# Norms moved to ScalarE, stores moved to the Sync queue, and weight fetches given out at each product's head

## The chip, the cores and the metric

The kernel runs on one core of one Trainium2 chip. Its engines are TensorE (PE, with PEld for the loading of weights), VectorE (DVE), ScalarE (ACT), GpSimd (POOL) and SyncE (SP). Each has its own in-order queue. DMAs are given out by SP, ACT or POOL, and an engine that gives one out first waits, in its queue, for what that DMA must wait for. The metric is the device time in microseconds of one launch.

## The reference

One block of a network on 4096 tokens of width 256, in float32: linear attention without a softmax, a residual and a layer norm, then a feed-forward part with a second residual and layer norm.

```
energy  = K^T V                       # 64 x 64, over all tokens
x1      = layernorm(x + (Q energy) * sqrt(3/64) @ wo^T)
h       = silu(x1 @ w1^T * s1) * (x1 @ w2^T * s2)        # 1024 wide
h       = gelu(h @ h1^T * hs1)                           # 1024 x 1024
h       = gelu(h @ h2^T * hs2)                           # 1024 x 1024
out     = layernorm(x1 + h @ w3^T * s3)
```

All the w and h matrices of the feed-forward part hold only -8, 0 and 8, which is what lets the kernel work with sums of their blocks without loss.

## The kernel before, in words

The tokens are eight tiles of 512, worked on in four pairs (p = 0 to 3). Values that need full precision are held as two parts, hi and lo (`convert`: a cast on ACT, L231, and a subtraction on DVE, L232), and every product is done once with each.

Stages. Keys, values and energy of all tiles come first, then queries. `stack` builds for each tile an operand `stk` of queries, hi over lo; for tiles 3 to 5 the lower half is made by `stack_lo` (L550) from a copy `qf`. Then tile 0 and tile 1 get their attention (`attention_out`, L137 and L138), the residual (`add`, L158), statistics, root and norm (`attend_norm`: `stats`, `root` with a power on POOL at L86, `norm` at L167), a turn on PE and the gate products (`gate_products`, L611; `gate`, L620 and L621), 16 gates through a ring of three pairs of banks. Gates 6, 7, 9 and 10 are followed by sums of blocks of h1; gates 11 and 14 by `add` for tiles 2 and 3, whose x comes from `load_x`.

Square layers (`square_layer`). Each of h1 and h2, times the 1024 x 1024 operand of a pair of tiles, is done with seven products of 512 x 512 in place of eight. A `product` is 32 matmuls (L278); it takes two half blocks of weights, `ws`, from a list `held`. The seven weight operands, in the order of use, are A11, A12, S2, S1, S3, A22, S4: three blocks of h and four sums of blocks (`sums`), which the kernel itself forms on DVE from raw blocks (`raw_blocks`) and stores (`store`, L440) to a scratch tensor `sw` in HBM. `fetch` keeps five half blocks in five rotating buffers, so a fetched block waits for the product that last read its buffer. In the first pair A11, A12 and A22 are fetched from h by POOL (L267, with a cast to the type of the products), the sums from `sw` by SP (L269); later pairs take all from `sw`, to which `copy` (L260) brings the A blocks.

Spare work is handed out by `fill`: after the third to sixth product of a layer it takes jobs from the list `background` until a budget in microseconds is used up (FILL; FIRST for the first layer of the first pair). In that first layer the jobs are the sums of h2 (`second_sums(k)`, k0 to k3, each two parts; the second part orders the raw block k+2), and for tiles 2 and 3 statistics, roots and norms on POOL (a0, a1 and b0, b1 of `attend_jobs`), then block transposes on DVE (L815; a2, a3 and b2, b3). A transposed tile is then moved block by block to `xT` by 32 DMAs a tile (`move`, L216), half on SP and half on POOL, 14 behind each product. Order written in the code is the order of each queue, as the schedule is manual.

After the two layers come the products with w3 (`last_products`, L755), the second residual (`take`), and the norm that goes to the output. A dummy activation `once` loads the table of Silu for the next pair's gates.

Of the kernel before, what the change touches and what calls it, by code (L numbers as in the profile page):

```python
# [11 lines left out]
F32 = mybir.dt.float32  # L12
# [9 lines left out]
P = 128  # L22
# [22 lines left out]
def block_kernel(ctx: ExitStack, tc: tile.TileContext, a: dict, out: bass.AP):  # L45
# [103 lines left out]
    def attend_norm(t, x, ps, pool):  # L149

        mv = p2.tile([P, NS, 2], F32, tag="mv1", name=f"mv1_{t}")
        y = pool.tile([P, NS, E], F32, tag=f"x2_{t // 2 % 2}", name=f"x2_{t}", bufs=2)
        r = {}
        x2[t] = y

        def add(g, j=slice(0, 2)):
            u = x[:, 2 * g : 2 * g + 2, :][:, j, :]
            nc.vector.tensor_tensor(u, u, ps[g][:, j, :], ALU.add)  # L158

        def stats(g):  # L160
            norm_stats([x[:, 2 * g + j, :] for j in range(2)], mv, 2 * g)

        def root(g):
            r[g] = rstd_of(p2, mv[:, 2 * g : 2 * g + 2, :], "a", 2)

        def norm(s, engine=nc.vector):
            engine.tensor_scalar(  # L167
                y[:, s, :], x[:, s, :], mv[:, s, 0:1],
                r[s // 2][:, s % 2 : s % 2 + 1], ALU.subtract, ALU.mult,
            )  # L170

        return add, stats, root, norm

    def turn_on_pe(t, slot):
# [61 lines left out]

    MOVES = 14
    FILL = {2: 2.0, 3: 4.0, 4: 1.5, 5: 3.5}
    FIRST = {2: 2.8, 3: 5.4, 4: 2.8, 5: 5.4}

    PLACE = {A11: (0, 0), A12: (HK, 0), A22: (HK, T)}
    ORDER = [A11, A12, S2, S1, S3, A22, S4]
# [27 lines left out]
            held.append(w)  # L270

    def product(ps, part, start):
        for h in range(2):
            w = held.popleft()
            for o in range(2):
                for k in range(HK):
                    for i in range(2):
                        nc.tensor.matmul(  # L278
                            ps[2 * h + o], w[:, k, o * P : (o + 1) * P], part[i][:, k, :],
                            start=start and k == 0 and i == 0, stop=k == HK - 1 and i == 1,  # L280
                            skip_group_check=True,
                        )
        fetch()
        products[0] += 1
        if products[0] in COPY:
            copy()
        move(MOVES)
# [5 lines left out]
    owed = [0.0]  # L293
    checks_due = [0]

    def fill(us):

        if checks_due[0] > 0:
            checks_due[0] -= 1
            check_job()  # L300
            us -= 1.4
        owed[0] = min(owed[0] + us, us)
        while background and owed[0] > 0:
            cost, job = background.popleft()
            owed[0] -= cost
            job()
        if not background:
            owed[0] = 0.0

    def square_layer(xb, first, sc, tail, spare):  # L310
# [58 lines left out]
        fill(spare[4])  # L369
        for o in range(HK):  # L370
            nc.scalar.copy(bb[:, o], al[o])  # L371
        for o in range(HK):
            c22(o)

# [2 lines left out]
        fill(spare[5])  # L377
        for o in range(HK):
            gelu(b5[:, o], al[o], HK + o)

        product(be, x22, False)
        n2 = convert(b5)
# [38 lines left out]
            )  # L421
        return d

    def sums(layer, k, raw):
        a11, a21, a12, a22 = (raw[:, i, :].bitcast(F32) for i in range(4))
        if layer == 0 and k < 2:

            so = [
                p1.tile([P, HK, T // 2], FR, tag="ws", name=f"so{layer}", bufs=HELD)
                .rearrange("p k o -> p (k o)").rearrange("p (m o) -> p m o", m=2)  # L430
                for _ in range(2)
            ]
        else:
            so = [
                p1.tile([P, 2, T], FR, tag="so", name=f"so{layer}", bufs=2) for _ in range(2)
            ]
        v = [s[:, i, :] for s in so for i in range(2)]

        def store(i):
            nc.gpsimd.dma_start(  # L440
                out=sw[layer][2 * i : 2 * i + 2, :, :, k, :].rearrange("m h p o -> p m h o"),
                in_=so[i].bitcast(F32).rearrange("p m (h o) -> p m h o", h=2),
            )

        def first():
            plus(v[0], a21, a22)
            plus(v[1], v[0].bitcast(F32), a11, ALU.subtract)
            store(0)

        def second():  # L450
            plus(v[2], a11, a21, ALU.subtract)
            plus(v[3], a12, v[1].bitcast(F32), ALU.subtract)
            store(1)

        return first, second
# [91 lines left out]
            nc.scalar.copy(qf[t][D:P], pq[t][D:P])  # L547

    def stack_lo(t):
        nc.gpsimd.tensor_tensor(  # L550
            stk[t][D:P], qf[t][D:P], stk[t][D:P].bitcast(F32), ALU.subtract
        )

# [3 lines left out]
    for t in range(NT):  # L557
        keys_values(t)
        if t > 0:
            energy(t - 1)  # L560
        if NT - 1 - EARLY <= t < NT - 1:
            queries(t - NT + 1 + EARLY)
            stack(t - NT + 1 + EARLY)
        if t >= NT - 4:
            if t % 2 == 0:
                early = sums(0, t // 2 - 2, raws[t // 2 - 2])
            early[t % 2]()
    queries(2, (0,))
    energy(NT - 1)
# [29 lines left out]
    split(0, 2)  # L599
    norm(2)  # L600
    norm(3)
    for t in range(3, LATE):
        stack_lo(t)
    for t in range(LATE, NT):
        stack(t)

# [19 lines left out]
    for o in range(3):  # L626
        for ps, w in zip(ring[o], (w1, w2)):
            gate_products(ps, w, o, slot, 0, slice(0, T // 2))
        if o == 1:
            turn(2, 4)  # L630
            split(2, 4)
    for o in range(3):
        for ps, w in zip(ring[o], (w1, w2)):
            gate_products(ps, w, o, slot, 0, slice(T // 2, T))
# [15 lines left out]
    for i in range(3, 2 * KH):  # L650
# [20 lines left out]
                later = sums(0, i // 3, raws[i // 3])  # L671
            later[i % 3]()
        if i == 7:
            raw_blocks(1, 0, xTr, nc.gpsimd)
            xs[2] = load_x(2)
            xs[3] = load_x(3)
        if i in (4, 14):
# [7 lines left out]
    def second_sums(k):  # L685
# [6 lines left out]
        def end():  # L692
            both[1]()
            if k + 2 < HK:
                raw_blocks(1, k + 2, later_raws[k % 2], nc.gpsimd)

        return [(1.4, begin), (1.4, end)]

# [101 lines left out]

        return [(1.3, functools.partial(half, s)) for s in (0, 2)]

    def attend_jobs(t):

        add, stats, root, norm = steps[t]

        def half(g):
            stats(g)
            root(g)
            for s in (2 * g, 2 * g + 1):  # L810
                norm(s, nc.gpsimd)

# [60 lines left out]
    for p in range(NP):  # L873
        ta, tb = 2 * p, 2 * p + 1
        if p > 0:
            first = []
            ask(1)
            for i in range(2 * KH):
# [21 lines left out]
                    fill(1.2)  # L900
                if p == NP - 1 and i in (11, 13, 15):
                    bounds((i - 11) // 2)
        if p + 1 < NP:
            (a0, a1), (a2, a3) = attend_jobs(ta + 2)
            (b0, b1), (b2, b3) = attend_jobs(tb + 2)
            if p == 0:
                k0, k1, k2, k3 = (second_sums(k) for k in range(HK))
                background.extend((*k0, *k1, a0, a1, *k2, *k3, b0, b1, a2, a3, b2, b3))
            else:
                background.extend((a0, a1, b0, b1, a2, a3, b2, b3))  # L910
        tail = lambda: None
        for layer, sc in enumerate((hs1, hs2)):
            if p + layer > 0:
                ask(4 if p else 1)
            if p == NP - 1 and layer == 1:
                background.append((1.4, functools.partial(bounds, 3)))
            xb, first, tail = square_layer(
                xb, first, sc, tail, FILL if p + layer else FIRST
            )
        while background:  # L920
            background.popleft()[1]()
        if p + 1 < NP:
            nc.scalar.activation(once, mhalf[:, :1], AF.Silu)

        made = {}

        for s in range(NS):
            last_products(0, first[0], s)
        move(MOVES)
        tail()  # L930
        made[2] = convert(xb[3])
        for s in range(NS):
            last_products(1, first[1], s)
# [231 lines left out]
```

## Time and profile before

| What | Value |
| --- | --- |
| median of 3 runs | 653.18 us (652.52 to 653.35) |
| the profiled execution, its own time | 653.67 us |
| its span, first to last instruction | 651.9 us |
| PE busy | 631.8 us (97%) |
| DVE busy | 496.1 us (76%) |
| ACT busy | 381.4 us (59%) |
| POOL busy | 233.1 us (36%) |
| PE's share of the chain of work that ended last | 86% |
| granted TensorE clock, mean | 0.987 |

In a row of the group table stand the line, the engine, the operation, what it writes from what, the count, then busy time and mean nanoseconds of one, then the idle time of the engine just before such instructions and what ended it. In the chain and the timelines a row is: start in us, length in us, what ran, and how many of them (a timeline adds the idle time before, in brackets). The chain is followed back from the last instruction, each time to what released it. Matmuls overlap, so their mean of 391 ns is longer than the distance between two of them.

### The profile page before, as it was taken

Reading aid. Unit: us, or ns where it says so; the run is one execution under the profiler, and the core shown is the slowest. Engines: PE = TensorE matmul, PEld = TensorE weight load, DVE = VectorE, ACT = ScalarE, POOL = GpSimd, SP = SyncE. Lnnn points to the kernel's source line nnn. Section 1 sums busy time; section 2 is a strip of 40 time slices with the busy share of each in tenths; the row PEclk is TensorE's granted clock in tenths of the full one; section 3 lists DMA queues with packets and bytes.
Section 4 is the critical chain, followed back from the end, with each engine's and each line's share of the span. In section 5 each row is a group of like instructions: output and inputs, shape, how many; then the busy total and the mean of one; then the engine's idle time right before and its main releaser. Section 6 shows DMA issues by size and latency. Waiting matters only on the chain.

```text
span 651.9 us, 8976 instructions
## 1 busy us (share of the span) xinstructions
PE 631.8 (97%) x3163; PEld 533.6 (82%) x3163; DVE 496.1 (76%) x750; ACT 381.4 (59%) x522; POOL 233.1 (36%) x290
## 2 busy tenths in 40 slices
PE   8999999959999999999999999999999999999994
PEld 7878888848898888888898888888899888888894
DVE  3789986895475888698677988798767987588466
ACT  5546472645664455655684556766684556766564
POOL 1234117722814713632535722631645720000005
PEclk9999999979999999999999999999999999999998
DMA  8988749845853037764762125654860125644201
GB/s 335 330 300 246 244 144 364 268 155 182 250 152 103 33 137 247 268 218 167 225 191 71 60 97 171 216 183 154 248 190 4 65 98 173 215 150 141 98 1 67
DMA packets 58800, 113.44 MB, mean 174 GB/s; under 512 B 19488, under 2 KB 34528, under 8 KB 58368
## 3 DMA queue, kind: packets, MB, share of 16 engines
q1 hardware_dynamic: 40864, 73.56, 34.0%
q0 software_dynamic: 17520, 38.55, 18.6%
q10 hardware_dynamic: 368, 0.72, 0.3%
q8 instruction: 26, 0.43, 0.3%
q14 instruction: 22, 0.18, 0.1%
HBM read 97.08 MB, written 18.87 MB: 178 GB/s over the span
## 4 chain that ended last, share of the span: by engine, by line
PE 86%; DMA 5%; DVE 5%; POOL 1%; issue 1%; ACT 1%; SPq 0%; POOLq 0%; DVEq 0%; ACTq 0%
PE bank L278 53%; PE bank L611 18%; PE bank L755 9%; DMA sw<-so 3%; PE bank L507 2%; DVE f L290 2%; PE bank L528 1%; DMA ws<-in_h 1%; POOL x L167 1%; DVE so L290 1%; DMA f<-in_xt 1%; PE bank L518 1%; PE bank L137 1%; PE bank L138 1%; DVE lo L232 1%
## 5 line engine op out<-in xcount | busy, mean ns | idle before, releaser
L278 PE MATMUL bank<-hi,ws 128*128 128x512 f32 x896 | 350.3, 391 | 7.7 <-DMA ws<-in_h 7.7
L278 PE MATMUL bank<-lo,ws 128*128 128x512 f32 x896 | 349.9, 391 | 0.0
L232 DVE TENSOR_TENSOR lo<-f,hi 128x1024 fp32r<-128x1024 f32 x144 | 170.3, 1221 | 69.6 <-ACT hi L231 69.1
L278 PEld LDWEIGHTS bank<-hi,ws 128*128 128x128 f32 x896 | 169.0, 189 | 43.3 <-DVE f L290 8.1
L278 PEld LDWEIGHTS bank<-lo,ws 128*128 128x128 f32 x896 | 169.1, 189 | 35.2
L231 ACT CAST hi<-f 128x1024 fp32r<-128x1024 f32 x144 | 144.5, 1051 | 52.0 <-PE bank L278 26.9
L318 ACT ACTIVATE f<-f,hs 128x512 f32<-128x512 f32 x96 | 62.8, 715 | 71.7 <-DVE f L290 71.7
L611 PE MATMUL bank<-hi,w 128*128 128x512 f32 (+1 forms) x268 | 101.7, 383 | 1.0 <-DVE d L766 0.6
L611 PE MATMUL bank<-lo,w 128*128 128x512 f32 (+1 forms) x268 | 101.2, 381 | 0.1
L620 ACT ACTIVATE f<-bank,s 128x512 f32<-128x512 f32 x64 | 44.0, 690 | 65.6 <-PE bank L611 62.3
L290 DVE TENSOR_TENSOR f<-f,f 128x1024 f32<-128x1024 f32 x64 | 76.5, 1221 | 4.5 <-ACT f L318 3.8
L290 DVE TENSOR_TENSOR f<-f,bank 128x512 f32<-128x512 f32 x96 | 62.1, 681 | 21.8 <-ACT f L371 16.0
L767 POOL TENSOR_TENSOR x<-x,d 128x256 f32<-128x256 f32 x31 | 27.0, 897 | 114.0 <-DVE d L766 113.9
L621 DVE SCALAR_TENSOR_TENSOR f<-bank,s,f 128x512 f32<-128x512 f32 x64 | 47.7, 748 | 26.2 <-PE bank L611 23.6
L755 PE MATMUL bank<-w,lo 128*128 128x256 f32 x256 | 61.6, 283 | 0.0
L755 PE MATMUL bank<-w,hi 128*128 128x256 f32 x256 | 61.6, 283 | 0.0
L611 PEld LDWEIGHTS bank<-hi,w 128*128 128x128 f32 x268 | 50.4, 188 | 11.3 <-DVE d L766 1.0
L611 PEld LDWEIGHTS bank<-lo,w 128*128 128x128 f32 x268 | 50.4, 188 | 9.6 <-DVE lo L191 0.3
L216 POOL DMA_DIRECT2D xT<-x x96 | 52.2, 551 | 8.1 <-DMA stage<-in_h 3.0
L755 PEld LDWEIGHTS bank<-w,lo 128*128 128x128 f32 x256 | 49.1, 192 | 0.2
L755 PEld LDWEIGHTS bank<-w,hi 128*128 128x128 f32 x256 | 49.1, 192 | 0.2
L717 POOL DMA_DIRECT2D stage<-in_h x16 | 9.0, 561 | 107.8 <-DVE stage L743 104.0
(121 smaller groups left out, 553.1 us busy)
## 6 DMA issues: line engine op xcount, KB each, us to landing
ws<-sw SPq DMA_DIRECT2D x100, 512.0 KB, 3.3
sw<-so POOLq DMA_DIRECT2D x16, 512.0 KB, 5.4
stage<-in_h POOLq DMA_DIRECT2D x16, 512.0 KB, 5.0
ws<-in_h POOLq DMA_DIRECT2D x12, 512.0 KB, 7.4
sw<-in_h SPq DMA_DIRECT2D x12, 512.0 KB, 5.5
x<-in_x SPq DMA_DIRECT2D x16, 256.0 KB, 3.7
f<-in_xt SPq DMA_DIRECT2D x6, 512.0 KB, 7.8
f<-in_h SPq DMA_DIRECT2D x6, 512.0 KB, 10.3
```

The lines of the kernel that those rows point to most:

```text
L216: moves.popleft()()
L231: nc.scalar.copy(hi[:, c, :], src[:, c, :])
L232: nc.vector.tensor_tensor(lo[:, c, :], src[:, c, :], hi[:, c, :].bitcast(F32), ALU.subtract)
L278: nc.tensor.matmul(ps[2 * h + o], w[:, k, o * P : (o + 1) * P], part[i][:, k, :], start=start and k == 0 and i == 0, stop=k == HK - 1 and ...
L290: engine.tensor_tensor(dst, u, v, op)
L318: nc.scalar.activation(dst, src, AF.Gelu, scale=sc[:, o : o + 1])
L507: nc.tensor.matmul(pk[:, s, :], x[:, k, s * P : (s + 1) * P], wkv[:, k, :], start=(k == 0), stop=(k == KE - 1),)
L611: nc.tensor.matmul(ps[:, c], w[:, k, o * P : (o + 1) * P], part[:, 2 * j + k, c], start=(k == 0 and i == 0), stop=(k == KE - 1 and i == 1),)
L620: nc.scalar.activation(g, pa, AF.Silu, scale=s1[:, o : o + 1])
L621: nc.vector.scalar_tensor_tensor(g, pb, s2[:, o : o + 1], g, ALU.mult, ALU.mult)
L755: nc.tensor.matmul(ps[:, :E], part[q][:, k, s * P : (s + 1) * P], w3[:, k0 + k, :], start=i % 2 == 0 and k == 0 and q == 0, stop=i % 2 == ...
L767: engine.tensor_tensor(y[:, s, :], y[:, s, :], d, ALU.add)
```

## The change

`norm` for tiles 2 and 3 is no longer two operations of POOL a half tile but, per 128 tokens, two activations on ACT: add minus the mean, then scale by the root. They are collected in `after_copies` and given out behind ACT's copies of the fifth product's banks, and behind the gelus of the sixth's. The roots stay on POOL. The transposes of tile 2 (a2, a3) move up into the fill of the fifth phase, before k3 and tile 3's statistics.

`fetch` moves from the end of a product to the head of the next one, so that the jobs, the copy and the moves between the two stand before it. The sums' stores go to SP, but for the two earliest, and so do the raw blocks of h2 for k = 0 and 2 (k = 1 and 3 stay on POOL). `stack_lo` goes from POOL to DVE, behind the second half of tile 0's split. In the first layer the jobs are listed by phase and not by a budget. The dummy Silu goes behind the `tail`, whose last gelu it stood ahead of.

```diff
+        def norm_on_act(minus):
+            for s in range(NS):
+                nc.scalar.activation(
+                    y[:, s, :], x[:, s, :], AF.Identity, bias=minus[:, s : s + 1], scale=1.0
+                )
+                nc.scalar.activation(
+                    y[:, s, :], y[:, s, :], AF.Identity, scale=r[s // 2][:, s % 2 : s % 2 + 1]
+                )
+        def minus_mean():
+            m = p2.tile([P, NS], F32, tag="mm", name=f"mm{t}")
+            nc.vector.tensor_scalar(m, mv[:, :, 0], -1.0, None, ALU.mult)
+            return m
...
     def product(ps, part, start):
+        fetch()
         for h in range(2):
             w = held.popleft()
...
-        fetch()
         products[0] += 1
         if products[0] in COPY:
             copy()
         move(MOVES)
...
+    after_copies = deque()
     def fill(us):
+        if isinstance(us, list):
+            for _, job in us:
+                job()
+            return
...
         for o in range(HK):
             nc.scalar.copy(bb[:, o], al[o])
+        while after_copies:
+            after_copies.popleft()()
...
             gelu(b5[:, o], al[o], HK + o)
+        while after_copies:
+            after_copies.popleft()()
...
-    def sums(layer, k, raw):
+    def sums(layer, k, raw, queue=nc.sync):
...
-            nc.gpsimd.dma_start(
+            queue.dma_start(
...
     def stack_lo(t):
-        nc.gpsimd.tensor_tensor(
+        nc.vector.tensor_tensor(
...
-                early = sums(0, t // 2 - 2, raws[t // 2 - 2])
+                early = sums(0, t // 2 - 2, raws[t // 2 - 2], nc.gpsimd)
...
-    for t in range(3, LATE):
-        stack_lo(t)
...
             split(2, 4)
+            for t in range(3, LATE):
+                stack_lo(t)
...
-            raw_blocks(1, 0, xTr, nc.gpsimd)
+            raw_blocks(1, 0, xTr)
...
-                raw_blocks(1, k + 2, later_raws[k % 2], nc.gpsimd)
+                raw_blocks(1, k + 2, later_raws[k % 2], (nc.sync, nc.gpsimd)[k % 2])
...
             root(g)
+            if on_act:
+                if g:
+                    norms, minus = norm.on_act
+                    after_copies.append(functools.partial(norms, minus()))
+                return
...
-                background.extend((*k0, *k1, a0, a1, *k2, *k3, b0, b1, a2, a3, b2, b3))
+                spare = {2: [*k0], 3: [*k1, a0, a1], 4: [*k2], 5: [a2, a3, *k3, b0, b1]}
+                background.extend((b2, b3))
...
-                xb, first, sc, tail, FILL if p + layer else FIRST
+                xb, first, sc, tail, FILL if layer else spare
             )
+        if p + 1 < NP:
+            fetch()
         while background:
             background.popleft()[1]()
-        if p + 1 < NP:
-            nc.scalar.activation(once, mhalf[:, :1], AF.Silu)
...
         tail()
+        if p + 1 < NP:
+            nc.scalar.activation(once, mhalf[:, :1], AF.Silu)
```

More of the change, by code (lines that the diff above doesn't have):

```diff
@@ L170, in norm @@
             )
+        def norm_on_act(minus):
[10 more added lines that the diff above has]
+            return m
+        norm.on_act = norm_on_act, minus_mean
         return add, stats, root, norm
@@ L238, in block_kernel @@
     FILL = {2: 2.0, 3: 4.0, 4: 1.5, 5: 3.5}
-    FIRST = {2: 2.8, 3: 5.4, 4: 2.8, 5: 5.4}
     PLACE = {A11: (0, 0), A12: (HK, 0), A22: (HK, T)}
@@ L801, in end_jobs, with attend_jobs @@
         return [(1.3, functools.partial(half, s)) for s in (0, 2)]
-    def attend_jobs(t):
+    def attend_jobs(t, on_act=False):
         add, stats, root, norm = steps[t]
@@ L902, in block_kernel @@
                     bounds((i - 11) // 2)
+        spare = FILL
         if p + 1 < NP:
-            (a0, a1), (a2, a3) = attend_jobs(ta + 2)
-            (b0, b1), (b2, b3) = attend_jobs(tb + 2)
+            (a0, a1), (a2, a3) = attend_jobs(ta + 2, p == 0)
+            (b0, b1), (b2, b3) = attend_jobs(tb + 2, p == 0)
             if p == 0:
                 k0, k1, k2, k3 = (second_sums(k) for k in range(HK))
-                background.extend((*k0, *k1, a0, a1, *k2, *k3, b0, b1, a2, a3, b2, b3))
+                spare = {2: [*k0], 3: [*k1, a0, a1], 4: [*k2], 5: [a2, a3, *k3, b0, b1]}
+                background.extend((b2, b3))
             else:
```

## The prediction

> **What bounds the kernel now.** I read the page's table of groups first, then the chain of work, then TensorE's clock by microsecond, then the order on GpSimd's queue. TensorE (PE) is busy 97% of the span, so only its idle time and its slow time can be won. The group of the square layers' products (L278) carries the largest idle time before it, and the chain shows where it lies:
>
> ```profile
> L278 PE MATMUL bank<-hi,ws 128*128 128x512 f32 x896 | 350.3, 391 | 7.7 <-DMA ws<-in_h 7.7
> ...
> 37.52 2.67 DVE x L167 x2
> 40.22 0.70 DVE stk L539
> ...
> 104.38 8.43 DMA sw<-so
> ...
> 125.02 0.73 POOL ra L86
> 125.85 3.83 POOL x L167 x2
> ...
> 134.19 7.89 DMA ws<-in_h
> ...
> 142.21 42.54 PE bank L278 x176
> ...
> 232.00 101.55 PE bank L278 x448
> ```
>
> One stop of 7.7 us, at 134.4: a weight block was issued at 134.19 by GpSimd (POOL) and landed 7.89 us later. POOL was late because two tiles' norms (L167) stood ahead of it. The last two lines give a second loss: 176 products in 42.54 us are 0.2417 us each, against 0.2267 undisturbed (101.55/448); 176 x 0.0150 = 2.6 us. The windows by microsecond (length, PE busy, clock, DMA share, GB/s) show why:
>
> ```profile
> 137.00:138.00 1.00, 0.00 (x0) 0.52 1.22 337
> ...
> 143.00:144.00 1.00, 1.00 (x3) 0.50 0.06 16
> ...
> 148.00:149.00 1.00, 1.00 (x6) 1.00 0.00 0
> ```
>
> The clock halves 2.6 us after PE stops and comes back 5 us after it resumes. Stop and slow clock are 10.3 us together. The first of four pairs of tiles is the only one with such a loss. POOL's timeline around it:
>
> ```profile
> 115.09 0.84 POOL L267 DMA_DIRECT2D ws<-in_h  x1
> 115.93 1.51 POOL L440 DMA_DIRECT2D sw<-so  x2
> 117.44 1.53 POOL L267 DMA_DIRECT2D ws<-in_h  x2
> 122.84 0.77 POOL L440 DMA_DIRECT2D sw<-so  x1 [3.88 <-DVE so L290]
> 124.08 0.76 POOL L440 DMA_DIRECT2D sw<-so  x1 [0.47 <-DVE so L290]
> 125.02 0.72 POOL L86 TENSOR_TENSOR ra<-ra,mhalf 128x2 f32<-128x2 f32 x1 [0.18 <-DVE ra L85]
> ```
>
> The reader is to see that POOL runs stores, roots and fetches strictly in turn.
>
> **What the Trainium skill says.** "TensorE: Matmul & The Clock Gate", section "What's actually happening": after an idle window of about 3.4 us the clock is halved, and about 3.4 us of work restore it. The trace agrees in kind; it took 2.6 and 5 us. "DMA: Bandwidth & Descriptors", "Queues, rings and completion order": a ring's descriptors are consumed in order, and each engine takes turns between rings; so a fetch behind stores on SP waits for their bytes too. The trace of before can't show this for stores on SP, as all went over POOL. "SBUF — State Buffer", "SBUF: two separate sides": VectorE (DVE) and GpSimd share a port pair, and the loser blocks. The trace agrees: L167 on DVE took 1.42 us beside stack_lo on POOL (37.4 to 41.3) and 0.41 us elsewhere.
>
> **The change part by part.** I number the first pair's products P1 to P14; undisturbed they start at 72.7 + 7.25(n-1), a second half 3.63 later.
>
> *Start, stack_lo to DVE.* Three operations leave POOL; on DVE they cost 3 x 0.65 (two of L539, the same shape, took 1.30) = 1.95 us. They fall after L191 at 42.3, where DVE has 1.24 + 0.21 + 0.44 = 1.89 us of idle time before 45.7: covered. Without that cover they would push the gates, whose slack I read as 0.2 to 0.3 us (gate 9 done 64.05, its bank pair wanted 64.37). In return L167 there falls from 2.75 to about 0.75 us, and PE's waits at 40.2 and 41.0 (0.74 + 0.18) go. Gain 0.9.
>
> *x loads behind stores.* Tiles 2 and 3 were loaded at 40.2 and 51.9. Now SP's order is two 512 KB stores (DVE gives them at 58.6 and 60.5), two 512 KB raw blocks, then x. From 60.4, 2.6 MB end with tile 2 and 3.15 MB with tile 3; at 0.31 to 0.35 MB/us (the 56 to 68 windows: 353, 290, 338 GB/s) that is 68 to 69 and 69.5 to 70.5. Tile 2 is added at 67.8, tile 3 at 71.0 (P1 needs its bank). I take a loss of 0.6, bounds 0 and 2.
>
> *Second sums' stores and half the raw blocks to SP; fetches at the head.* A fetch now follows the earlier product's fill jobs. S3's second half comes behind 2.1 MB issued from 95.6; with A22's first block, 2.85 MB from 96 at 0.33 gives about 105.3, and P5 wants it at 105.3: loss 0.5, bounds 0 and 1.5. A22's second half goes behind POOL's raw block and two roots: issue 106 to 107.6, landing about 112.5, wanted 112.5; what it stops PE there is taken off the next stop.
>
> *Norms on ScalarE (ACT).* POOL loses 8 x 1.4 to 1.9 us. ACT gets 16 operations; the end's L958 and L959, the same two, take 0.495 and 0.507 and a pair starts every 0.97 us, so 3.9 us a tile. Tile 2's run from 109.8 to 113.7 in the 5.0 us that ACT waited before its gelus at 114.8: covered. Tile 3's wait for DVE's statistics at 126.1 and end about 130.1; queued behind them is the conversion of the next operand, hi at 131.1, lo at 132.3, wanted by P9 at 130.7. Alone this costs 1.6 us; the next item delays P9 past it, so it counts as nothing.
>
> *Where the stall goes.* POOL's order is now A11's first block, the two roots of tile 3, A11's second, A12's first, seven moves, A12's second. Those roots need DVE: n1's lo until 119.8, four transposes now ahead (0.36 each, 1.4), the sums k3 (2.6), statistics (2.2): 126.1, as before, since the transposes use up what DVE saves on store waits. The second root ends at 126.9, so A11's second block leaves about ten microseconds after its 117.4 of before. Landing took 4.3 us when alone and 7.4 to 8.0 in company; I take 5, as only the last k3 store and the block behind it are with it: 132.0 against 127.05 wanted by P8's second half. Stop 4.95, plus the 0.5 of P5. The clock very likely halves: 3.4 to 5 us at half rate, 2.0. A12's second block waits for the landing of A12's first, eight DMAs back on POOL's lanes (about 134.3), and lands at 139.5 to 142; P9's second half comes at 141.6: 0.4. Together 4.95 + 0.5 + 2.0 + 0.4 = 7.85 in place of 10.3. Gain 2.5.
>
> *End of the first pair.* The xT moves were late (ACT waited 6.9 for them) and PE lost 0.6 at 202.0 behind DVE; tile 3's moves now go in P12 to P14. Gain 0.6. *Silu after the tail* removes two table loads a pair, 3 x 2.6 us of ACT (1.28 each); PE runs through there (15.35 us of L755 without a gap), so nothing. Later pairs: L278 already runs 448 in 101.55 without a wait; seven moves (0.6 each) ahead of a fetch stay under its lead of over 10 us. Nothing.
>
> Sum: 0.9 - 0.6 + 2.5 + 0.6 = 3.4. The profiled execution took 653.67 with a span of 651.9, 0.5 above the median of 653.18; span 648.5, median 649.8.
>
> **The rivals.** A difference of 0.2%, 1.3 us, is about what a measurement of this kernel can tell from none.
>
> (a) The stall moves to P8's second half, as above: 649.8, own range 647.7 to 651.8. For it: the order of POOL's queue. Chance 0.57.
>
> (b) The same place, shorter: A11's second block lands within 4.3 us and PE's stop stays too short for the clock to fall; 2.0 + 0.7 less: 647.1. Against: 7.7 us of stop halved it after 2.6. 0.12.
>
> (c) No stall is left: 653.2 - 10.3 - 0.9 - 0.6 = 641.4. Against: the roots before A11's second block would have to end by 122. 0.05.
>
> (d) A chain of slow fetches: A11's second lands 8 us after its issue (134.9), A12's second 7.9 after A12's first (136 + 7.9 = 143.9). P9's second half then starts as late as before's 142.2 and the slow clock together (144.8) but for 0.9; with the 0.5 lost ahead and 0.9 from start and end net, 652.0 to 653. 0.17.
>
> (e) Slower: x for tile 3 late. Every microsecond past 71.3 stops the whole PE before P1. Against (a)'s 3.4 and the 0.6 counted, it decides for slower from 5.3 us on, a landing at 76.6, when SP's ring would have moved 3.15 MB at 195 GB/s. Slices with small packets ran near that (214 over 94 to 102). 654.5 or more. 0.09.
>
> **How the numbers follow.** Faster: (a), (b), (c) = 0.74; within: (d) 0.17; slower: (e) 0.09. The likeliest is 649.8. The range runs from 646.0 (into (b), leaving (c)) to 653.4 (through (d), leaving (e)).
>
> **What would show it.** A stop on L278 of 4 to 6 us at about 128, released by a ws<-in_h DMA issued right after a root (L86); half clock behind it; no POOL norms before 190; L167 near 37 at 0.4 us; ACT's norms of tile 3 waiting for DVE's mean near 126. Wrong would be: no PE wait between P7 and P9 (then (c)), or PE or DVE waiting for x near 69 to 72 by more than 2 us (then (e)).

## The result and the profile after

The changed kernel is slower. It took 654.36 us (median of 20 runs, 652.29 to 656.26) against 651.84 us for the kernel before (20 runs, 649.58 to 655.11): a ratio of 1.0034, interval 1.0022 to 1.0047. A second measurement gave 1.0034 again (1.0015 to 1.0053). The forecast was 3.4 us faster; 2.3 to 2.5 us slower came out, outside the range.

The profiled execution took 655.52 us with a span of 653.7. Its group table and the chain of work that ended last (start, length, what ran) answer to the lines shown of before:

```profile
L295 PE MATMUL bank<-hi,ws 128*128 128x512 f32 x896 | 350.3, 391 | 5.9 <-DMA ws<-in_h 3.5
...
63.56 6.99 DMA x<-in_x
...
104.85 10.30 DMA sw<-so
...
154.83 29.30 PE bank L295 x128
...
230.51 101.55 PE bank L295 x448
```

The one stop of 7.7 us is gone, but 5.9 us of idle time remain before the same products (L278 is now L295). The load of x (6.99 us) has come into the chain, and a store to `sw` of 10.30 us stands where one of 8.43 us stood. The list of waits (who waited for whom: us in all, how many, the longest) splits most of the 5.9 (issue: released by nothing that the profile shows):

```profile
PE bank L295 <- DMA ws<-in_h: 3.5, 2, 2.8
PE bank L295 <- DMA ws<-sw: 1.6, 1, 1.6
PE bank L295 <- issue: 0.6, 1, 0.6
```

None of these is at P8's second half, where I had put the stop. The 1.6 us are at P5's second half (S3), the 2.8 at P6's second half (A22). GpSimd's timeline shows why A22 is late:

```profile
104.52 1.13 POOL L444 DMA_DIRECT2D stk<-in_h  x2 [8.07 <-DVE so L306]
...
107.12 1.60 POOL L86 TENSOR_TENSOR ra<-ra,mhalf 128x2 f32<-128x2 f32 x1 [0.35 <-DVE mm L184]
108.68 0.78 POOL L282 DMA_DIRECT2D ws<-in_h  x1
...
129.91 1.52 POOL L282 DMA_DIRECT2D ws<-in_h  x2
```

The half block issued at 108.68, behind two raw blocks and two roots, landed 9.4 us later, and TensorE, which waits for it, goes on at 118.26. The windows by microsecond (length, busy time and count of PE, PEld, DVE, ACT and POOL, clock, DMA share, GB/s) show what it met on the way, and that the clock halves again:

```profile
116.00:117.00 1.00, 0.00 (x0) 0.00 (x0) 1.00 (x3) 0.34 (x1) 0.00 (x0) 1.00 1.28 364
...
119.00:120.00 1.00, 1.00 (x4) 0.77 (x3) 0.00 (x0) 1.00 (x3) 0.00 (x0) 0.50 1.10 331
```

The first pair is then about as long as before, not longer (the table below). The loss is behind the last product. Here is the stretch from the last product with w3 to the end of the span, first of before:

```profile
643.18:651.90 8.72, 0.47 (x5) 0.16 (x3) 3.79 (x17) 2.43 (x5) 1.44 (x3) 0.64 0.27 95
```

and of after:

```profile
641.69:653.70 12.01, 0.47 (x5) 0.16 (x3) 3.79 (x17) 2.43 (x5) 1.44 (x3) 0.60 0.19 69
```

The same instructions with the same busy time take 3.3 us more. The records of the sequencers, which the page's groups don't list, show where: GpSimd closes with three DRAINs, and the first of them is long. It begins 3.61 us after the last product in both, and the engines' last instructions stand behind its end. The rows give shortest, median and longest in nanoseconds, first of before:

```profile
L1160 POOLq DRAIN  x3: 46/103/4273, 646.8 to 651.6; - x3
```

and of after:

```profile
L1194 POOLq DRAIN  x3: 46/103/7618, 645.3 to 653.5; - x3
```

The long one, called the DRAIN or the last DRAIN from here on, grew by 3.35 us, which is the whole difference.

To see what is chance I took further profiles, four of before and three of after in all. Microseconds by stage, from the starts of TensorE's instructions:

```
stage                                before (4)                      after (3)              mean difference
span's start to 65th product         15.52 18.82 15.28 18.55         17.01 15.25 17.31      chance
65th product to P1                   57.14 57.12 57.11 57.14         56.32 55.65 56.95      -0.82
P1 to last product of first pair     111.70 109.90 109.58 109.96     110.42 110.25 110.06   -0.04
from there to the next pair's first  47.47 47.73 47.49 48.07         46.61 46.61 46.60      -1.08
from there to last product with w3   411.34 in all                   411.34 in all           0.00
from there to the span's end         8.70 in all                     12.05 in all           +3.35
```

The sum without the start is +1.41 us, or 0.22%, at the lower end of the first measured interval and inside the second. The start, which the change doesn't touch, moves by 3.6 us from execution to execution. About 1 us of the 2.3 to 2.5 us measured is thus in no stage of these means; seven profiles are too few to say whether it is chance, and it stays open.

### The profile page after: what moved, and what is told of

The parts are those of the page before. It is cut to its first block, busy times and chain, and to the rows that moved or that the text cites. A ratio compares the mean times of both kernels' runs of the same rounds, so it can differ in the third digit from the quotient of the medians.

```text
span 653.7 us, 8984 instructions
## 1 busy us (share of the span) xinstructions
PE 633.9 (97%) x3163; PEld 534.7 (82%) x3163; DVE 496.1 (76%) x755; ACT 380.4 (58%) x532; POOL 205.1 (31%) x263
## 4 chain that ended last, share of the span: by engine, by line
PE 83%; DVE 7%; DMA 4%; ACT 2%; issue 2%; SPq 0%; POOLq 0%; POOL 0%; DVEq 0%; ACTq 0%
PE bank L295 52%; PE bank L635 15%; PE bank L781 9%; PE bank L533 3%; DMA sw<-so 2%; DVE f L306 2%; DVE so L306 1%; PE bank L554 1%; DVE lo L248 1%; DMA x<-in_x 1%; ACT f L340 1%; DVE f L645 1%; PE bank L544 1%; DMA f<-in_xt 1%; ACT hi L247 1%
## 5 line engine op out<-in xcount | busy, mean ns | idle before, releaser
L295 PE MATMUL bank<-hi,ws 128*128 128x512 f32 x896 | 350.3, 391 | 5.9 <-DMA ws<-in_h 3.5
L295 PE MATMUL bank<-lo,ws 128*128 128x512 f32 x896 | 349.6, 390 | 0.0
L295 PEld LDWEIGHTS bank<-hi,ws 128*128 128x128 f32 x896 | 168.7, 188 | 43.4 <-issue 4.2
L295 PEld LDWEIGHTS bank<-lo,ws 128*128 128x128 f32 x896 | 168.7, 188 | 35.0
```

The source lines that it names most:

```text
L295: nc.tensor.matmul(ps[2 * h + o], w[:, k, o * P : (o + 1) * P], part[i][:, k, :], start=start and k == 0 and i == 0, stop=k == HK - 1 and ...
```

## The experiments

Four questions: does the tail belong to the change or to chance; what made the new stops; what sets the DRAIN; and does the tail turn the sign. P1 to P14 are numbered as in the prediction. Ratios are to before, measured beside each run. Closing time means: from the last product with w3 to the end of the execution's own time (before 8.70 + 1.79 = 10.49 us, after 12.05 + 1.79 = 13.84).

**Both kernels again.** No edit.

> The kernel before, unchanged: a second profile, to tell chance from the change in two places where the first pair of profiles differ and no edit is in sight: the start (kv products 32 to 63 slow in after's profile, first to 65th product 9.67 before against 10.16 us) and the end (GpSimd's last DRAIN, 4.27 us before against 7.62 after; last product to end of span 8.7 against 12.05 us). Theory T1 (the change itself makes the DRAIN longer): DRAIN 4.3 again within 0.5, tail 8.5 to 9. Theory T2 (the DRAIN varies by chance): a DRAIN anywhere from 4 to 8 us. Both expect one PE stop of 7 to 8 us at the eighth product.

> The changed kernel, unchanged: a second profile. T1: DRAIN 7.6 again within 0.5, tail about 12. T2: another value between 4 and 8. The start under both: the 65th product between 15.5 and 17.0. The stops in the first pair under both: one of about 2.8 us in the sixth product (A22's first block) and one of 1.6 in the fifth (S3's); if these vary by more than 1 us, landing times are chance too.

> The kernel before, a third profile: how much of the spread of its times (648 to 656) is the start, and how much the stop at the eighth product. Seen so far: first to 65th product 10.2 and 12.2 us, stop 8.1 and 6.3 us with the clock at half for 10.2 and 6.8. If the stop is the same each time, first to last product of the first pair is 109.9 to 111.7 again; if it is chance, a value under 109 shows in an execution whose time is under 652.

> The kernel before, a fourth profile, as for the third: first pair 109.9 to 111.7 again, or less where the time is under 652. Tail 8.70 and DRAIN 4.27 again.

DRAIN and tail are the program's own: the DRAIN took 4.272 to 4.273 us in four profiles of before, 7.618 to 7.620 in three of after (the third with after_3, below). For the tail chance is ruled out. (By the count of matmuls the stop of before, put at the eighth product above, is at P9's second half, and the block that P6 waits for in after is A22's second.) Before's stop is not the same each time, and the profile that I predicted from was its longest. The waits of the third profile of before:

```profile
PE bank L278 <- DMA ws<-in_h: 5.4, 1, 5.4
```

5.4 in place of 7.7 us, with 6.83 us of half clock in place of 10.24: the first pair took 109.58 us and the execution 651.28. The fourth (655.56) had nearly the same first pair, 109.96, but its 65th product came 3.27 us later, so most of the spread is the start.

**The fetch back at the product's end.**

```diff
     def product(ps, part, start):
-        fetch()
         for h in range(2):
...
+        fetch()
         products[0] += 1
```

> After, with the fetch put back at a product's end, ahead of the copy, the moves and the jobs; all else of the change stays. If the fetch's place behind the jobs is what leaves the stops at the fifth and sixth product and the slow clock behind them: no stop over 1 us among P1 to P14, first to last product of the first pair about 103 instead of 110.4 us, and 6 to 8 us less than after. If the stops come from the stores' bytes on SP, whatever the place of the fetch: the S3 stop stays (1 to 2 us), the A22 one goes, 3 to 5 us less. If the norms on ScalarE were all that was worth anything and A22's block behind two roots on GpSimd is the cause, also 3 to 5 less. GpSimd's DRAIN at the end: T1 expects 7.6 as in after (the fetch's place changes no DMA count).

655.09 us (653.07 to 658.28), ratio 1.0059 (1.0038 to 1.0080): no gain. The stops at P5 and P6 did go, A22's second half block being issued at 97.09. But TensorE then stopped at P9. Its timeline, ScalarE's and VectorE's (idle before in brackets):

```profile
129.04 0.39 PE L294 MATMUL bank<-lo,ws 128*128 128x512 f32 x1
134.80 0.76 PE L294 MATMUL bank<-hi,ws 128*128 128x512 f32 x1 [5.37 <-issue]
...
126.78 0.51 ACT L175 ACTIVATE x<-x,mm 128x256 f32<-128x256 f32 x1 [5.38 <-DVE mm L184]
...
130.68 1.97 ACT L247 CAST hi<-f 128x1024 fp32r<-128x1024 f32 x2
...
131.74 2.36 DVE L248 TENSOR_TENSOR lo<-f,hi 128x1024 fp32r<-128x1024 f32 x2 [4.99 <-ACT hi L247]
134.02 1.88 DVE L306 TENSOR_TENSOR f<-f,bank 128x512 f32<-128x512 f32 x3
```

Read upwards: P9 writes the banks that P7 filled; VectorE's additions (134.02) read the first of them just before P9 starts at 134.80; they stand behind `lo`, that behind `hi` on ScalarE, and that behind tile 3's eight norms, which themselves waited for VectorE's mean until 126.78. So what P9 needs is late by tile 3's statistics on VectorE and the norms on ScalarE behind them. In after this is covered only because P5 and P6 have already put P9 back to 138.1.

**The stores and raw blocks back on GpSimd.**

```diff
-    def sums(layer, k, raw, queue=nc.sync):
+    def sums(layer, k, raw, queue=nc.gpsimd):
...
-            raw_blocks(1, 0, xTr)
+            raw_blocks(1, 0, xTr, nc.gpsimd)
...
-                raw_blocks(1, k + 2, later_raws[k % 2], (nc.sync, nc.gpsimd)[k % 2])
+                raw_blocks(1, k + 2, later_raws[k % 2], nc.gpsimd)
```

> After, with the sums' stores and all raw blocks of h2 back on GpSimd; norms on ScalarE, the fetch at a product's head and the rest of the change stay. T1: the DRAIN follows what GpSimd gave out and is 4.3 us again, tail 8.7 instead of 12.05. T2: no pattern. In the first pair: S3's block no longer queues behind stores on SP, so the 1.6 us stop at the fifth product goes; GpSimd gets 12 stores more at 0.75 us, so A22's first block (108.7 in after) is issued 1 to 3 us later and the stop at the sixth product grows from 2.8 to 4 to 6 us. Net against after: 3.35 less from the tail, 1.6 less and 1 to 3 more from the stops: 2 to 4 us less under T1, and 1 to 3 more under T2.

650.65 us, ratio 0.9980 (0.9966 to 0.9995): faster than before. S3's wait is gone (its second block was issued at 91.32, with no store ahead of it on Sync, where after had 100.60); A22's is 4.0 us, as said:

```profile
PE bank L295 <- DMA ws<-in_h: 4.0, 1, 4.0
```

The first pair fell to 108.62 us. From the 65th product to P1 it was 55.59 us, 0.72 less than after's mean: what x behind the stores cost. (All twelve profiles here that have the stores on Sync up to P1 took 55.56 to 56.95 us, 56.15 on the mean; the four with the stores on GpSimd 55.57 to 55.60. That makes it 0.57.) The DRAIN was 3.13 us, yet the tail 10.76: Sync's closing waits now stood still for 2.5 us with nothing in the record but a fetch of instructions (its queue moved a block 0.85 us after the waits stopped, and 1.65 us later they went on). By the stages that is 0.72 + 1.62 (first pair) + 1.29 (closing) = 3.6 us less than after, and by the ratios 3.5, so that the stages, the closing among them, account for this difference.

**Tile 3's norms put off to the second layer**, on top of the fetch at the product's end; the second run also has stores and raw blocks on GpSimd.

```diff
-                spare = {2: [*k0], 3: [*k1, a0, a1], 4: [*k2], 5: [a2, a3, *k3, b0, b1]}
-                background.extend((b2, b3))
+                spare = {2: [*k0], 3: [*k1, a0, a1], 4: [*k2], 5: [a2, a3, *k3]}
+                spare2 = {2: [(1.4, due_check), b0], 3: [b1], 4: [b2, b3], 5: [], "late": True}
...
-                xb, first, sc, tail, FILL if layer else spare
+                xb, first, sc, tail, (spare2 if p == 0 else FILL) if layer else spare
...
         fill(spare[3])
+        while "late" in spare and after_copies:
+            after_copies.popleft()()
```

`due_check` is a job that `fill` otherwise puts first by itself.

> The run before with the fetch at a product's end (fetch_end), and besides tile 3's statistics, roots and ScalarE norms put off to the second layer's third and fourth phase (its transposes to the fifth). Theory A (the step of the prediction that cost tile 3's norms at nothing was the failure: they hold the ninth product's operand back, 5.8 us of stop and 6.8 us of half clock in fetch_end): no stop over 1 us in P1 to P14 and no half clock before the end; first to last product of the first pair 101.5 to 103.5 us instead of 110.2; 7 to 9 us less than fetch_end. Theory B (a weight block, A12's second half behind the roots, is what P9 waits for anyway): with the roots gone from in front of it this goes too, so the trace of fetch_end (lo of the operand done at 134.1, P9 at 134.8) is what speaks against it; B alone would leave a stop of 4 us or more at P9. DRAIN at the end: 7.62 as in after under the theory that GpSimd's own list of instructions sets it.

> norms_late with the sums' stores and raw blocks of h2 back on GpSimd. Under theory A the first pair is as good as in norms_late if GpSimd, free of norms and of the roots of tile 3, gives its fetches out in time: 101.5 to 104.5 us. DRAIN as in stores_pool: 3.1 us, tail 10.8 instead of 12.05, so 1.3 us less than norms_late at most; if the stores' own issues (0.75 us each) make a fetch late, 1 to 3 us more than norms_late.

652.55 us (ratio 1.0007, 0.9991 to 1.0024) and 646.09 us (0.9924, 0.9898 to 0.9951). P9's stop is gone in both, so theory A holds for P9, with one limit: the runs put off tile 3's statistics, roots and norms together, and that the norms are the step that counts is read from the timeline above. My figures were missed: the first pair took 106.56 and 106.12 us (101.5 to 104.5 expected), and the first run was 3.4 us faster than fetch_end by the ratios (7 to 9 expected). I had put the norms ahead of the copies (L399) that free P13's banks, as ScalarE's timeline of the second run shows:

```profile
158.58 0.51 ACT L178 ACTIVATE x<-x,ra 128x256 f32<-128x256 f32 x1
159.00 1.97 ACT L247 CAST hi<-f 128x1024 fp32r<-128x1024 f32 x2
160.88 2.03 ACT L399 COPY f<-bank 128x512 f32<-128x512 f32 x4
```

P13 started at 161.50 instead of 158.8. The two runs differ in their closing time by 13.83 - 10.17 = 3.66 us and in the rest of the traces, without the start, by 1.1 us; their medians, on one chip, by 6.5. Part of the remainder is that the first run's profile lies 2.5 us under its median (650.01); why the medians differ by so much stays open.

**Tile 3's norms behind those copies**, otherwise the second run, and the same norms with the fetch at the head and the stores on Sync.

```diff
-                spare2 = {2: [(1.4, due_check), b0], 3: [b1], 4: [b2, b3], 5: [], "late": True}
+                spare2 = {2: [(1.4, due_check), b0], 3: [b1], 4: [], 5: [b2, b3]}
...
-        while "late" in spare and after_copies:
-            after_copies.popleft()()
```

> norms_late_pool with tile 3's norms in ScalarE's queue behind the copies of the second layer's fifth product instead of ahead of them. There they held up the copies that free the banks of the 13th product: a stop of 2.9 us and 3.4 us of half clock. Expected: no stop over 1 us in P1 to P14, no half clock before the end; first to last product of the first pair 101.5 to 102.5 us instead of 106.1; DRAIN 3.1, tail 8.4; the end of the first pair up to 1 us longer, as tile 3's transposes come a phase later. Against norms_late_pool 3 to 5 us less, 641 to 643. If another wait takes the place of this one: a stop elsewhere between P10 and P14 and no gain.

> After, with tile 3's statistics, roots and norms put off to the second layer as in norms_fifth_pool, but with the fetch still at a product's head and the stores on Sync. If the fetch's place behind the jobs is what makes S3's and A22's blocks late: the stops of 1.6 to 2.5 us at the fifth and of 2.8 to 3.0 at the sixth product stay, with 3.4 us of half clock; what follows them has no stop over 1.1; the first pair 107 to 109 instead of 110.3. If the norms were behind these stops too: no stops, 102.

The first took 644.18 us, ratio 0.9880 (0.9852 to 0.9908). Its first pair runs through; group row and chain:

```profile
L294 PE MATMUL bank<-hi,ws 128*128 128x512 f32 x896 | 348.8, 389 | 0.0
...
72.75 101.77 PE bank L294 x448
```

That is 8.7 us less in the first pair than after. The second run (one execution, 651.91 us) kept the stops at P5 and P6 (waits of 1.5 and 2.6 us, 6.83 us of half clock; first pair 108.83), so they don't come from tile 3's norms. P6's stop went with the fetch at the product's end (fetch_end) and stayed with the stores on GpSimd (stores_pool): it comes from the fetch's place. P5's went in either case: it takes the fetch's place and the stores on Sync together.

**What sets the DRAIN.** All four are after with one edit: block moves of later tiles taken from Sync to GpSimd, or small operations added to GpSimd.

```diff
-                            (nc.sync, nc.gpsimd)[len(moves) % 2].dma_start,
+                            (nc.gpsimd if t == 4 else (nc.sync, nc.gpsimd)[len(moves) % 2]).dma_start,
```

(t in (4, 5) for ring32, (4, 5, 6) for ring48), and for drain_ops

```diff
         made = {}
+        if p == 1:
+            few = p1.tile([P, 2], F32, tag="few", name="few")
+            nc.gpsimd.memset(few, 1.0)
+            for _ in range(16):
+                nc.gpsimd.tensor_tensor(few, few, few, ALU.mult)
```

> After, with all 32 block moves of tile 4 given out by GpSimd instead of 16 of them: 16 DMAs more on GpSimd (165 as in before), long before the end. If GpSimd's last DRAIN goes with the number of DMAs it gave out: the DRAIN falls from 7.62 to about 4.3 or 3.1 us, tail 8.7 to 10.8 instead of 12.05. If it goes with its other instructions or with when things happen: 7.62 again, within 0.1. Nothing else in the time should change by more than 0.5.

> After, with 17 tiny operations more on GpSimd (a memset and 16 multiplications of 128x2 elements on a tile of its own) after the second pair's square layers, where GpSimd is idle. If GpSimd's last DRAIN goes with the number of its DMAs: 7.62 again, within 0.1. If it goes with the number of its instructions, whatever they are: another value, by some microseconds. No other effect.

> After, with all block moves of tiles 4 and 5 given out by GpSimd: 32 DMAs of 32 packets more on its queue than in after, 16240 packets in place of 15216. Theory R (GpSimd's last DRAIN takes about 2.6 ns for each packet of its queue since the count last passed a multiple of 4096; worked out from 7.62 us at 15216 = 3 x 4096 + 2928 and 8.93 us at 15728): 16240 = 3 x 4096 + 3952, a DRAIN of 10.3 us, tail from the last product 14.7 us. Rival (each such DMA adds 0.08 us, without end): also about 10.2. Rival (the kinds of DMAs decide, not their packets): no number.

> After, with all block moves of tiles 4, 5 and 6 given out by GpSimd: 48 DMAs more than in after, 16752 packets = 4 x 4096 + 368. Theory R: the count has passed the next multiple of 4096, so the DRAIN falls to about 1.0 us (up to 1.3[...]), and the tail, then set by Sync's closing waits, to 8.4 instead of 12.05 us; the first pair as in after (110.3); so 3.6 us less than after, 650 to 651, and that is the change without its tail: 1 to 2 us faster than before. Rival (growth without end): 11.5 us of DRAIN, 4 us slower than after.

From the sequencers' records, with two later runs:

```
kernel                           GpSimd's DMAs   DRAIN us   tail us   closing us
before                           165             4.27       8.70      10.49
after, fetch_end, head_fifth     149             7.62       12.05     13.84
drain_ops (17 operations more)   149             7.62       12.05     13.84
drain_dma (16 moves more)        165             8.93       13.36     15.15
ring32 (32 more)                 181             1.58       8.30      12.14
ring_spread (32 more)            181             1.58       10.64     12.42
ring_spread_40 (40 more)         189             2.23       8.25      12.99
ring48 (48 more)                 197             2.89       8.26      10.04
norms_late                       149             7.62       12.05     13.83
stores_pool                      165             3.13       10.76     12.55
norms_late_pool                  165             3.13       8.39      10.17
norms_fifth_pool                 165             3.13       10.73     12.51
fifth_moves (16 moves fewer)     149             1.82       8.38      10.16
```

Seventeen more operations of GpSimd left the DRAIN as it was. Each block move more adds 0.082 us (four pairs of rows: 1.31 for 16 twice, 1.31 fewer for 16 fewer, 0.65 for 8), and once, between 16 and 32 moves more, the DRAIN falls back by 8.65 us (7.62 + 2.61 - 1.58). So it rises and falls back, and the count of DMAs alone does not set it. My first guesses (fewer for more DMAs; packets modulo 4096, which gave 10.3 and 1.0 for ring32 and ring48) were wrong; that DMAs move it and that it falls back held. The law itself stays open: before and stores_pool give out the same DMAs on GpSimd in another order and differ by 1.14 us. A rival is not told apart either: every move that joined GpSimd's queue left Sync's, so no run changes the one count alone. ring48 took 654.91 us (ratio 1.0039, 1.0022 to 1.0056) in spite of its short closing: 32 moves a tile in one queue were late, and the third pair began 2.0 us later for it. Its first pair took 111.48 us, with stops at P5, P6 and P8; no move that the edit touches is in there, so that is chance. The others were single executions: drain_dma 656.43, drain_ops 653.63 and ring32 659.90 us, whose third pair began 6.5 us later.

**Does the tail turn the sign?** The added moves spread over four tiles, and after itself on the same chip.

```diff
-                            (nc.sync, nc.gpsimd)[len(moves) % 2].dma_start,
+                            (nc.sync, nc.gpsimd)[len(moves) % 4 > 0 if t > 3 else len(moves) % 2].dma_start,
```

(for ring_spread_40 the condition is `len(moves) % 16 not in (0, 5, 10) if t > 3`)

> After, with 24 of the 32 block moves of each of tiles 4 to 7 given out by GpSimd in place of 16: the same 32 DMAs more as ring32, but spread over four tiles, so that none of them is late. DRAIN 1.58 us as in ring32, tail 8.3 instead of 12.05 us; last product of the first pair to the first of the second and so on as in after (46.6 us, not 53.2 as in ring32's third). If the longer closing tail is what makes after slower: 3.7 us less than after, so 650 to 651.2 beside 652 to 652.5 for before, a ratio under 1. If after's loss has another cause and the closing time is made up elsewhere in it: 653 or more.

> ring_spread with 26 in place of 24 of the 32 block moves of tiles 4 to 7 on GpSimd, 40 DMAs more than in after; eight DMAs fewer on Sync, so that its closing waits no longer stand still as they did in ring_spread (10.64 us of tail with a DRAIN of 1.58). Expected: DRAIN 1.58 + 8 x 0.082 = 2.2 us, tail 8.3 against 12.05, first pair 110 as in after, 46.6 behind it. If the longer tail alone turns the sign: 3 to 4 us less than after on the same chip, and a ratio to before of 0.997 to 0.9995. If after is slower for another reason: a ratio over 1.001.

> The changed kernel beside it on the same chip, to have both ratios from one set of runs of before: 1.002 to 1.005 as first measured, tail 12.05, DRAIN 7.62, first pair 110.2 to 110.5.

The DRAINs came out as expected (1.58 and 2.23), the closing time didn't. ring_spread was held by Sync's waits (tail 10.64). In ring_spread_40 the tail was 8.25, but 4.74 us lie between its span and its own time (652.97 against 648.2) where all but ring32 have 1.79; fetches of instructions are recorded there, 2.6 to 3.1 us after the last instruction. So of 3.7 to 3.8 us only 1.42 and 0.85 were saved. Measured: 652.96 us, ratio 1.0023 (1.0002 to 1.0045), and 652.85 us, 1.0019 (1.0003 to 1.0035), beside after_3's 653.87 us, 1.0034. That is 0.7 and 1.0 us less than after, of the size of what was saved, but the intervals overlap. By the terms set beforehand both ratios fall on the side of another cause; as most of the closing time was still there, they don't decide it. A kernel after with a closing as short as before's was not had. That its sign would turn is a sum, not a measurement: 1.41 - 3.35 = -1.94 us by the stages, 2.3 to 2.5 less 3.35 = about -1 us by the medians.

**The same lever on the best kernel.** norms_fifth_pool with 16 moves fewer on GpSimd:

```diff
+                            (nc.sync, nc.gpsimd)[len(moves) % 8 in (1, 3, 5) if t > 3 else len(moves) % 2].dma_start,
```

> norms_fifth_pool with 12 in place of 16 block moves of each of tiles 4 to 7 on GpSimd and 20 on Sync. Its tail was 10.73 us though its DRAIN was 3.13, as Sync's closing waits stood still for 2.5 us with nothing to wait for but a fetch of instructions in the record; norms_late_pool, with the same DRAIN and one instruction more on Sync, had 8.39. Sixteen DMAs more on Sync move the place of that fetch. Expected: DRAIN 1.8 (3.13 less 1.31), tail 8.3 and 2.3 us less than norms_fifth_pool if Sync is not caught by such a fetch; 10.7 again if the fetch falls there whatever the count. First pair 101.5 as there.

642.31 us (640.73 to 643.62), ratio 0.9854 (0.9820 to 0.9888): the best of all, 1.5% under before. DRAIN 1.82 and tail 8.38 as expected. Its closing is 2.35 us shorter than norms_fifth_pool's, its first pair 0.38 longer (101.92), and its fourth pair begins 0.71 us later; the ratio fell by 0.0026, 1.7 us, with intervals that overlap. Its chain has one short break in the first pair:

```profile
72.97 72.54 PE bank L294 x320
145.82 29.30 PE bank L294 x128
```

## Why the prediction was wrong

Two terms failed: the end, which the sum put at nothing and which cost 3.35 us, and the stall, which was to give 2.5 us and gave none.

*What the sum left out: the end.* "Later pairs ... Nothing" was right for the products (411.34 us in both), but the sum ended with the last product. The change took 16 DMAs off GpSimd, and GpSimd's closing DRAIN went from 4.27 to 7.62 us. Without this term of +3.35 us the stages add up to -1.94. I had counted what the moved DMAs cost on their queues, and not that the engine they left still has to close. The profile before shows the DRAIN, but not what would change it.

*Where the stall goes* (gain 2.5, the largest term): nothing was gained; the first pair is 110.29 us in before's profiles and 110.24 in after's. (The runs with moves of later tiles and drain_ops have after's instructions up to the end of that pair; with them it is nine profiles, 109.57 to 111.48 us, 110.33 on the mean.) Two steps failed. The first was the size of what goes away: 10.3 us came from one profile, whose half clock was one step longer than in the other three; the mean loss against 101.32 is 9.0. The second was the place. I said of A22's second half: issue 106 to 107.6, landing about 112.5, wanted 112.5. It was issued at 108.68 and TensorE went on at 118.26. I gave it about 5 us on the way with a megabyte of raw blocks issued just ahead of it in its own queue and stores on Sync, while the DMA engines moved about 360 GB/s (348 to 373 in the windows from 114 to 119). The profile before had shown this: the same half block, issued there at 98.95 right behind two raw blocks, took 10.0 us, which "4.3 us when alone and 7.4 to 8.0 in company" leaves out. Its rows in GpSimd's timeline and its time to landing:

```profile
97.86 1.10 POOL L418 DMA_DIRECT2D xT<-in_h  x2
98.95 0.77 POOL L267 DMA_DIRECT2D ws<-in_h  x1
...
DMA to landing us min/median/max: 10.0/10.0/10.0
```

That stop (2.8 us, half clock behind it), with S3's (0.5 forecast with bounds 0 and 1.5; 1.0 to 2.3 by the three profiles) and smaller ones at P9 and after, cost what before's had cost. A11's second block was then only just early enough: issued at 129.91 (forecast 127), it landed at 134.16, and P8's second half, put back by the earlier stops, began at 134.46. Without them it would have been wanted at 127.7. So the stop forecast at P8 was covered, not wrong in kind: in drain_dma, whose first pair is the same program and where P6 happened not to stop, A11's second block was issued at 129.55 and P8's second half waited 3.4 us for it, with 3.41 us of half clock behind.

*Norms on ScalarE, "counts as nothing" since P9 is late anyway:* true in after, and for the reason given, only that other stops made P9 late. fetch_end showed the cover gone: a 5.8 us stop and 6.83 us of half clock, where I had priced 1.6 us. The norms began at 126.78 and ended at 130.77, near the forecast; I had followed the operand of P9 and not the additions queued behind it on VectorE that free P9's banks.

*stack_lo and L167, gain 0.9:* right in kind, too small. Before's 57.13 us to P1 became 55.59 in stores_pool, which keeps this edit and takes the stores out of x's way: 1.54. L167 fell from 2.75 to 0.73 us, and `stack_lo` ran on VectorE in 1.90 us, under cover.

*x behind the stores, loss 0.6:* right; 0.72 by after's three profiles, 0.57 by all sixteen.

*End of the first pair, gain 0.6:* right in kind, 1.08. *Silu, nothing:* right.

The rivals: (b) and (c) didn't occur. The sign set for (c), no wait between P7 and P9, did show in after, yet the stall had not gone; it stood at P5 and P6. (d), slow fetches in a chain, had the nearer price for a fetch, 7.9 to 8 us against the 9.4 measured, but at other blocks; (e) didn't decide. No rival looked at the end.

## What to carry to other kernels

Put the program's closing into the sum: compare the stretch behind the last useful instruction as well, and when DMAs move from one engine's queue to another, GpSimd's closing DRAIN and Sync's closing waits may change by microseconds that no view of the product stages shows. Take a stall's size from several profiles of the kernel before, and the time of a fetch from one that had the same company. And when work moves into an engine's idle time, follow everything queued behind it to the banks and buffers that it frees: here the places of tile 3's norms and of the fetch were worth 1.0% (ratio 0.998 of stores_pool to 0.988 of norms_fifth_pool), several times what the change as made moved.

## What the runs showed of the hardware

- GpSimd's long closing DRAIN took 1.58 to 8.93 us, the same to 2 ns in the repeated profiles of one program (four of before, three of after). It rose by 0.082 us for each 16 KB block move taken from Sync to GpSimd and fell back once by 8.65 us; that the fall recurs is not shown.
- Sync's closing waits stood still for 2.5 us in stores_pool (tail 10.76) and not in norms_late_pool (8.39), which has two instructions more on Sync in the record. That a fetch of instructions holds them is argued from its time, and from fifth_moves, where other counts removed it; it is not shown.
- Wherever the clock fell in the first pair it was at half for 3.41 us or for two or three times that (6.83, 10.24); in norms_late, norms_fifth_pool and fifth_moves it never fell there. Counted from the start of the matmul ahead to that of the one behind, stops of 2.0 to 4.5 us cost none or one such step (two in head_fifth, after 3.0 us), stops of 5.8 to 8.1 us two or three.
- 512 KB weight blocks on GpSimd's queue took 3.8 to 4.3 us at the quickest, 10.0 us behind two raw blocks in before, and 9.4 us behind two in after with about 360 GB/s moving; the store on Sync beside the last took 10.3.
